# Attention, convolution and two MLPs on one core: scores made one unit ahead in the last groups, with six other moves of loads and fillers

## The chip, the cores and the metric

The kernel runs on 1 core of a Trainium2 chip, in one launch. The metric is the device time of that launch in microseconds (us), the median of several runs. Everything is in 32-bit floats.

## What is computed

The input is two images of 56 x 56 tokens with 384 channels. Two blocks follow one another; the reference, cut to what matters:

```python
# block 0: neighbourhood attention (12 heads of 32, 7 x 7 keys for each query), then an MLP
h = neighborhood_attention(layer_norm(x), w_qkv, b_qkv, rpb, w_proj, b_proj)
x = x + h
x = x + gelu(layer_norm(x) @ w1 + b1) @ w2 + b2            # 384 -> 1536 -> 384
# block 1: convolution and scans, then an MLP
p = layer_norm(x) @ w_in + b_in                            # 384 -> 768
local = conv3x3_depthwise(p)
mixed = 0.25 * (lr + rl + tb + bt) + local                 # four running means: decay 0.6, gain 0.4
x = x + layer_norm(mixed) @ w_out + b_out
x = x + gelu(layer_norm(x) @ w1 + b1) @ w2 + b2
```

The scores get a table of position biases (`rpb`) before the softmax, with a very negative value at every key outside a query's 7 x 7.

## The kernel before

**Engines and queues.** The order of the instructions is written out by hand, and each engine runs its own in that order. PE is TensorE, DVE VectorE, ACT ScalarE, POOL GpSimd. All transfers are issued by SP (`nc.sync`), in program order: an issue that has to wait for a semaphore holds all later ones.

**Start.** The first 448 tokens are loaded in four parts, normalized by DVE (L226), turned by PE (L357) and taken to SBUF by ACT (L362); then keys, values and queries are made (L386, L424). PSUM banks come from `any_bank`, four in turn.

**Attention.** The tokens lie in 14 groups of 8 rows (7 for an image), and a group in 4 windows of 14 columns (`Window`). A window's 12 heads are done in 3 units of 4 heads (`Unit`), so the loop has 168 steps `s`, 12 for a group (`n` is the group, `k` the step in it). The keys of a window are cut into 2 chunks at the image's edges (in the first and last group of an image, and in the first and last window of any) and into 3 elsewhere. For a unit with `m` chunks:

- `scores` (L515): 4 `m` matmuls, each recorded twice, into `sc`, two tiles of two banks, one bank for each head. A unit fills 112 `m` of a bank's 512 columns;
- `biased` (L530, DVE): adds the bias in two halves of two heads, from the banks to `pts`; `numerators` (L536, ACT) takes the exponential;
- `gathered` (L546, L548, DVE): adds the chunks for the sums, left out from group 12 on (`END`), where PE sums them instead;
- `values` (L556, L563): two steps later, values and sums into `o` and `sums`;
- for each window: `take` (L478, ACT), `gather` (L482), `invert` (L488 to L494) and `divide` (L498, L500).

Where two 2-chunk units follow one another, both are scored in one burst in the first one's step, the second at column 224, and nothing is scored in the second's step; else a unit is scored in its own step.

PE's time in a step is filled up with other matmuls, "fillers": queries, keys and values of later groups (`ahead`, L386 and L424) and projections of finished tokens (`project`, L582). A filler's bank is emptied at the start of the next step (`take` on ACT, or the add L590 on DVE). `spare` names the steps of a group that get no filler from `ahead`: 3, 4 and 5 where there are nine such jobs, which is so in group 11 (`END - 1`); that group gets no projections either. In groups 12 and 13 seven projections stand at steps written out in `THEN`; seven more come after the last unit.

**Loads of attention.** `Window` loads its values `vt` (L465) one window ahead. `load_bias` (L316) loads a table when the place changes, into one buffer for each of three kinds; 18 times in all. `load_residual` (L571) loads a tile of `x` for the residual into one of three `xr` buffers, so the load waits for the store of the tile three before; POOL adds the shift (L576), after `steps` steps or when the projection's add needs it. In the last 16 steps six parts of the first MLP's weights are loaded (L625), 768 KB each. At `s == NU`, behind the last unit, come the loads of the first two groups of `x1` (L609) and the last four residual tiles.

**MLPs and mixing** (`passes`). Block 0's MLP and block 1's input projection run group by group; `Beside` hands out convolution and scans on DVE in small steps between PE's work. Scans along the columns (`Columns`, one job for each image and channel block) add to `mix_d` in DRAM. The second pass (`dgroups`) loads a group of `mix_d` and `x2` (`load_mix`, L1274), measures it for the normalization during the hidden layer (`measure`, L1288: PE turns, DVE takes the statistics), and projects it out. `beside.until(name)` hands out DVE's jobs up to that one. Group 6 (`half_way`) is the first with tokens of image 1. Its load waits for the last job `(1, NI - 1)`, is cut into pieces of 128 tokens with all 6 channel blocks, and its tile `k` is measured in step 2 `k` + 3 of the 12 of the hidden layer (L1080) before.

Of the kernel before, what the change touches and what calls it, by code (L numbers as in the profile page):

```python
# [41 lines left out]
NH, KS, HD = 12, 7, 32  # L42
P = 128
NC = C // P
INNER, NI = 2 * C, 2 * C // P
HID, NHID = 4 * C, 4 * C // P
TT = 112
# [3 lines left out]
T1, T2 = H * W, B * H * W  # L51
# [122 lines left out]
def block_kernel(ctx: ExitStack, tc: tile.TileContext, ins: dict, out: bass.AP):  # L174
    nc = tc.nc
# [11 lines left out]
    mix_d = [dram.tile([NI, P, H * W], F32, name=f"mix_d{b}") for b in range(B)]  # L187
# [119 lines left out]
    def load_bias(n, j):  # L307

        b, g = groups_a[n]
        pr, pc = place(g, NG), place(j, NWC)  # L310
        if (b, pr, pc) in biases:
            return
        _, at, size = BIAS_T_AT[pr, pc]
        most = NH * TT * (3 if pc == 1 else 2)
        t = kp.tile([P, most], F32, name=f"bias{pc}")
        nc.sync.dma_start(out=t[:, :size], in_=ins["bias_t"][:, at : at + size])  # L316
        biases[b, pr, pc] = t[:, :size].rearrange("p (n c q) -> p n c q", n=NH, q=TT)

    load_x(0)
# [59 lines left out]
    def any_bank():  # L379

        return ps_s.tile([P, GT], F32, name="ps", tag="any")
# [186 lines left out]
    def load_residual(t, pool=lp, bufs=3, steps=4):  # L568

        xrs[t] = pool.tile([P, C], F32, name="xr", bufs=bufs)  # L570
        nc.sync.dma_start(out=xrs[t], in_=xf[t * P : (t + 1) * P, :])  # L571
        loaded[t] = steps
# [33 lines left out]
    def load_group(src, group, tag):  # L606
        t0, n = group
        t = xp.tile([P, NT, C], F32, name=tag)
        nc.sync.dma_start(  # L609
            out=t[:, :n, :], in_=src[t0 : t0 + n * P, :].rearrange("(k p) c -> p k c", p=P)  # L610
        )
        return t

    def weights(layer):

        w1 = wm.tile([P, NC, HID], F32, name=f"w1_{layer}", tag="w1")
        w2 = wm.tile([P, NHID, C], F32, name=f"w2_{layer}", tag="w2")
        s1 = ins[f"L{layer}_conv_w1"].rearrange("(c p) n -> p c n", p=P)
        s2 = ins[f"L{layer}_conv_w2"].rearrange("(c p) n -> p c n", p=P)
        parts = []  # L620
        for h in range(0, HID, HID // 3):
            parts.append((w1[:, :, h : h + HID // 3], s1[:, :, h : h + HID // 3]))
        for c in range(0, NHID, NHID // 3):
            parts.append((w2[:, c : c + NHID // 3, :], s2[:, c : c + NHID // 3, :]))
        return w1, w2, [lambda d=d, s=s: nc.sync.dma_start(out=d, in_=s) for d, s in parts]  # L625

    def norm_of(x, n, small):
        norm = Norm(small)
# [13 lines left out]
            nc.sync.dma_start(out=dst, in_=src)  # L642


    tps = [any_bank() for c in range(NC)]
    halves = [Norm(sm) for h in range(2)]
    for h, norm in enumerate(halves):
# [39 lines left out]
        channels_of(2, c, any_bank)()  # L687
    load_bias(0, 3)
    for t in range(3):
        load_residual(t)  # L690
    shift_by_values(ep, ps_t, wproj, shift)
    sctx.close()

# [13 lines left out]
    for s in range(NU + 4):  # L707
        n, k, hg, i = s // UG, s % UG, s % NC, s // NC
        if s == NU:

            kctx.close()
            xp = ctx.enter_context(tc.tile_pool(name="x", bufs=2, side="right", reuse_waits="tile"))
            tail_pool = actx.enter_context(tc.tile_pool(name="a_tail", bufs=1))
            xs = {g: load_group(x1f, groups[g], "xa") for g in range(2)}
            for t in range(T2 // P - 4, T2 // P):
                load_residual(t, tail_pool, 4, 2)
        store_all()
        while load:
            load_residual(load.pop(0))
        if k == 0 and n < ng:  # L720
            vals = []
            if n + 1 < ng:
                ahead += [lambda n=n, m=m: query_or_key(n + 1, m, one_bank) for m in range(NC)]
                vals += tiles_of(n + 1)[2:]
            if n + 2 < ng:
                vals += tiles_of(n + 2)[:2]
            ahead += [lambda t=t: value(t, one_bank) for t in vals]
            if n + 2 < ng:
                ahead += [
                    lambda n=n, m=m: query_or_key(n + 2, m, one_bank) for m in range(NC, 2 * NC)  # L730
                ]

            spare = (3, 4, 5) if len(ahead) == 9 else (4, 6)

        if k == 2 and n + 4 < ng:
            load_x(n + 4)
# [8 lines left out]
        if s < NU and hg == 2 and s + 1 < NU:  # L745
            ws[i + 1] = Window(i + 1)
        if s >= NU - UG - 4 and hg == 2 and w_parts:
            w_parts.pop(0)()

        if s <= NU:  # L750
            for take in taking:
# [5 lines left out]
        if s < NU:  # L757

            if s not in units:
                units[s] = Unit(ws[i], hg)  # L760
                units[s].scores()
                behind = Unit(ws[(s + 1) // NC], (s + 1) % NC) if s + 1 < NU else None
                if behind is not None and (units[s].m + behind.m) * TT <= BANK:
                    behind.scores(units[s].m)
                    units[s + 1] = behind
        new, before, last = units.get(s), units.get(s - 1), units.pop(s - 2, None)
        done = last.w if last is not None and last.hg == NC - 1 else None
# [203 lines left out]
    def passes(xs, xn, w1, w2, between=lambda ps: None):  # L971
# [14 lines left out]
        def images(t, n):  # L986


            for b in range(B):
                lo, hi = max(t, b * T1), min(t + n, (b + 1) * T1)  # L990
                if lo < hi:
                    yield b, lo - b * T1, lo - t, hi - lo
# [273 lines left out]
        def load_mix(g):  # L1266
            t0, n = dgroups[g]
            mx = io.tile([P, NI, MT], F32, name="mx")

            step = P if g == half_way else n * P  # L1270
            for t in range(0, n * P, step):
                for b, at, here, size in images(t0 + t, step):
                    here += t
                    nc.sync.dma_start(  # L1274
                        out=mx[:, :, here : here + size],
                        in_=mix_d[b][:, :, at : at + size].rearrange("m p t -> p m t"),
                    )
            x = load_group(x2_d, dgroups[g], "xa")
            if g >= half_way:
                add_row(x, dgroups[g][1], "b_out")  # L1280
            return mx, x, Norm(sm)

        def measure(mx, norm, k):
            parts = []
            for h in range(2):
                ps = ps_t.tile([P, NC, P], F32, name="xi", tag="pt")
                for c in range(NC):
                    nc.tensor.transpose(  # L1288
                        ps[:, c, :], mx[:, h * NC + c, k * P : (k + 1) * P], ident
                    )  # L1290
                parts.append(ps.rearrange("p c q -> p (c q)"))
            norm.add(k, parts)
# [12 lines left out]
        def measure_beside(m, g, ahead):  # L1305


            n = dgroups[g][1]
            if g > half_way:
                if m % 2 == 0 and m // 2 < n:  # L1310
                    measure_by_vector(ahead[0], ahead[2], m // 2)
            elif m % 2 == 1 and 0 < m // 2 <= n:
                measure(ahead[0], ahead[2], m // 2 - 1)
            if m == 10:
                ahead[2].close(n)

        def project_out(g, mx, x, inner):
# [174 lines left out]
        for g, (t0, n) in enumerate(dgroups):  # L1492
# [37 lines left out]
                    add_row(x3, dgroups[g + 1][1], "b2_1")  # L1530
                beside.go(ROW_D)
            if g + 2 == half_way:
                beside.until((1, NI - 1))
                ahead = load_mix(g + 2)
        pctx.close()

# [90 lines left out]
```

## Time and profile before

| | |
|---|---|
| median of 3 runs | 2680.19 us (2678.64 to 2681.08) |
| profiled execution | 2680.04 us, span 2678.2 us |
| PE busy | 2640.3 us (99%) |
| DVE busy | 1963.2 us (73%) |
| ACT busy | 898.7 us (34%) |
| POOL busy | 249.7 us (9%) |
| DMA | 299 MB, mean 112 GB/s |
| PE idle in 0 to 20 us | 7.46 us |
| PE idle in 570 to 710 us | 14.1 us |
| PE idle in 2110 to 2140 us | 7.66 us |

Times in the profile are from the span's start. A group of the profile reads: line, engine, operation, output<-inputs, count, busy time, and the idle time before it with what ended it. Ends of matmuls are modelled, so a stall within a burst shows as a longer burst. "PEclk" is the share of TensorE's full clock that was granted.

### The profile page before, as it was taken

What the parts mean: (1) busy time and instruction counts of PE and PEld (TensorE: products, weight loads), DVE (VectorE), ACT (ScalarE), POOL (GpSimd) and SP (SyncE); (2) the same over time, 40 slices, a digit from 0 to 9 for tenths busy, and PEclk for the clock granted to TensorE, in tenths of its full rate; (3) what the DMA queues carried; (4) which work ended last, traced back from release to release, by engine and by line L of the source; (5) the groups of instructions that cost most, each with busy time, mean ns of one, the idle gap of its engine ahead of it and who ended that gap; (6) DMA issues with size and microseconds to landing.
All of it is one profiled execution on the core that took longest, in us unless ns stands there. A gap on an engine that the chain in (4) does not pass through costs nothing. (4 is left out here: it accounts for less than half of the span.)

```text
span 2678.2 us, 37275 instructions
## 1 busy us (share of the span) xinstructions
PE 2640.3 (99%) x14963; PEld 1473.9 (55%) x14963; DVE 1963.2 (73%) x3539; ACT 898.7 (34%) x1447; POOL 249.7 (9%) x264
## 2 busy tenths in 40 slices
PE   8999999999899999999999999999999899999999
PEld 4666666656655455555555555555555455555556
DVE  3778877876365698688989889888988627677652
ACT  4555555554322332223344422311143211111111
POOL 1111111111211100000010000000010011101100
PEclk9999999999999999999999999999999999999999
DMA  6323454224411132233346544533346401111000
GB/s 216 134 89 102 154 170 146 80 77 158 156 37 38 65 107 88 89 128 105 123 156 230 184 149 150 178 120 114 118 182 228 152 19 37 45 44 39 30 12 17
DMA packets 134249, 298.99 MB, mean 112 GB/s; under 512 B 11463, under 2 KB 89905, under 8 KB 131761
## 3 DMA queue, kind: packets, MB, share of 16 engines
q1 hardware_dynamic: 134064, 296.50, 32.3%
q8 instruction: 119, 1.95, 0.3%
q14 instruction: 66, 0.53, 0.1%
HBM read 180.86 MB, written 115.61 MB: 111 GB/s over the span
## 5 line engine op out<-in xcount | busy, mean ns | idle before, releaser
L1080 PE MATMUL mm<-hT,w 128*128 128x512 f32 (+2 forms) x1872 | 771.1, 569 | 0.4 <-ACT hT L254 0.2
L1080 PEld LDWEIGHTS mm<-hT,w 128*128 128x128 f32 x1872 | 352.7, 190 | 383.5 <-issue 352.1
L1089 ACT ACTIVATE hid<-mm,chan 128x512 f32<-128x512 f32 (+2 forms) x312 | 206.1, 661 | 683.3 <-PE mm L1080 683.2
L1096 PE MATMUL y_end<-w,hid 128*128 128x384 f32 x1200 | 395.2, 486 | 0.0
L1174 DVE SCALAR_TENSOR_TENSOR loc<-pt,taps,loc 128x990 f32<-128x990 f32 (+9 forms) x336 | 377.1, 1122 | 10.0 <-ACT loc L1156 1.7
L1096 PE MATMUL y<-w,hid 128*128 128x384 f32 x1152 | 379.4, 486 | 0.0
L1096 PEld LDWEIGHTS y_end<-w,hid 128*128 128x128 f32 x1200 | 227.5, 190 | 157.2
L1096 PEld LDWEIGHTS y<-w,hid 128*128 128x128 f32 x1152 | 218.2, 190 | 150.5 <-issue 1.0
L530 DVE TENSOR_TENSOR pts<-sc,bias 119x448 f32<-119x448 f32 (+3 forms) x336 | 220.9, 699 | 78.2 <-PE sc L515 75.2
L536 ACT ACTIVATE pts<-pts 119x448 f32<-119x448 f32 (+3 forms) x336 | 206.8, 642 | 191.3 <-DVE pts L530 187.9
L222 POOL TENSOR_TENSOR rs<-rs,mhalf 128x4 f32<-128x4 f32 (+4 forms) x67 | 87.1, 1300 | 1727.0 <-DVE rs L219 1691.6
L386 PE MATMUL ps<-hT,wqkv 128*128 128x448 f32 x504 | 212.0, 559 | 2.0 <-ACT qT L396 0.7
L1064 DVE STREAM_TRANSPOSE hT<-xn 32x96 f32<-32x96 f32 x672 | 181.1, 269 | 31.4 <-PE mm L1080 11.8
L1080 PE MATMUL mm<-hT,w_in 128*128 128x512 f32 (+2 forms) x468 | 191.9, 568 | 0.6 <-ACT hT L254 0.6
L240 ACT ACTIVATE xn<-xc,sh,rs 128x384 f32<-128x384 f32 x98 | 64.7, 698 | 268.6 <-DVE sh L233 268.5
L1080 PEld LDWEIGHTS mm<-hT,w_in 128*128 128x128 f32 x468 | 88.5, 190 | 102.1 <-issue 90.6
L386 PEld LDWEIGHTS ps<-hT,wqkv 128*128 128x128 f32 x504 | 90.2, 191 | 82.8 <-issue 73.1
L515 PEld LDWEIGHTS sc<-qT,kT 32*100 32x100 f32 (+3 forms) x3168 | 91.6, 170 | 67.1 <-issue 17.9
L1299 DVE STREAM_TRANSPOSE turned<-mx 32x192 f32<-32x192 f32 x336 | 123.3, 367 | 4.2
L515 PE MATMUL sc<-qT,kT 32*100 32x112 f32 (+3 forms) x3168 | 114.7, 272 | 6.5 <-DVE pts L530 5.8
L556 PE MATMUL o<-pts,vt 100*32 100x112 f32 (+3 forms) x3168 | 112.7, 266 | 3.8 <-DMA vt<-v_d 2.7
L582 PE MATMUL ps<-wproj,og 128*128 128x384 f32 x294 | 107.1, 503 | 3.6 <-DVE xr L590 3.6
(104 smaller groups left out, 2644.9 us busy)
## 6 DMA issues: line engine op xcount, KB each, us to landing
bias<-in_bias_t SPq DMA_DIRECT2D x16, 1344.0 KB
loc<-loc_d SPq DMA_DIRECT2D x24, 784.0 KB
mixed<-mix_d SPq DMA_DIRECT2D x24, 784.0 KB
mix_d<-mixed SPq DMA_DIRECT2D x24, 784.0 KB
xa<-x_d SPq DMA_DIRECT2D x22, 768.0 KB
p_d<-mx SPq DMA_DIRECT2D x10, 1536.0 KB
mx<-mix_d SPq DMA_DIRECT2D x10, 1536.0 KB
pt<-p_d SPq DMA_DIRECT2D x18, 560.0 KB
```

The costliest lines, as they stand in the source:

```text
L386: nc.tensor.matmul(ps, lhsT=wqkv[:, c, m * P : (m + 1) * P], rhs=hT[:, c, half_of(n)], start=c == 0, stop=c == NC - 1,)
L515: nc.tensor.matmul(sc[i // 2][: w.keys, i % 2, (first + c) * TT : (first + c + 1) * TT], lhsT=kT[d, hg, w.keys_at + r * w.kc : w.keys_at + ...
L530: nc.vector.tensor_tensor(self.of(half), sc[half][:n, :, at].rearrange("p h (c q) -> p h c q", q=TT), self.w.bias[:n, 4 * self.hg + h : 4 ...
L536: nc.scalar.activation(self.of(half), self.of(half), AF.Exp)
L556: nc.tensor.matmul(o[i * HD : (i + 1) * HD, hg, :], lhsT=w.vt[:n, c, h * HD : (h + 1) * HD], rhs=self.pts[:n, i, c, :], start=c == 0, stop ...
L582: nc.tensor.matmul(ps, lhsT=ogs[t // 7][:, c, at : at + P], rhs=wproj[:, c, :], start=c == 0, stop=c == NC - 1,)
L1064: nc.vector.transpose(hT[j : j + HD, :, k * P + i : k * P + i + HD], xn[i : i + HD, k, :].rearrange("p (c q) -> p c q", c=NC)[:, :, j : j ...
L1080: nc.tensor.matmul(ps[:, : n * P], lhsT=w[:, c, m * P : (m + 1) * P], rhs=hT[:, c, : n * P], start=c == 0, stop=c == NC - 1,)
L1089: nc.scalar.activation(t[:, : n * P], ps[:, : n * P], AF.Gelu, bias=col(b1, m))
L1096: nc.tensor.matmul(ps, lhsT=t[:, k * P : (k + 1) * P], rhs=w[:, m, :], start=m == 0, stop=m == len(lhs) - 1,)
L1174: nc.vector.scalar_tensor_tensor(to, pt[:, lo + dy - self.top : hi + dy - self.top, xt : xt + n], self.tap(dy, dx), to, ALU.mult, ALU.add,)
L1299: nc.vector.transpose(t[j : j + HD].rearrange("p (m c) -> p m c", m=NI)[:, :, i : i + HD], mx[i : i + HD, :, k * P + j : k * P + j + HD],)
```

## The change

- Bias tables of all groups but the first are issued by ACT (`nc.scalar`) instead of SP, and so are the six parts of the first MLP's weights.
- Twelve matmuls of `ident` stand at PE's start; their result is not used.
- The first three residual tiles get their shift after 8 steps instead of 4.
- At `s == NU` two residual tiles come ahead of each of the two groups of `x1`, which were first.
- In group 11 `spare` is (3, 6, 9).
- From group 12 on, a step whose unit has its scores makes those of the next one, in the half of the banks that its own unit does not take (where both have 2 chunks).
- The half-way group's mixture is loaded in two parts: five channel blocks once the last but one job is done, the sixth after the last. Its tiles are measured two steps later, and its statistics closed at step 11 instead of 10.

```diff
@@ -313,7 +313,8 @@
         _, at, size = BIAS_T_AT[pr, pc]
         most = NH * TT * (3 if pc == 1 else 2)
         t = kp.tile([P, most], F32, name=f"bias{pc}")
-        nc.sync.dma_start(out=t[:, :size], in_=ins["bias_t"][:, at : at + size])
+        queue = nc.sync if n == 0 else nc.scalar
+        queue.dma_start(out=t[:, :size], in_=ins["bias_t"][:, at : at + size])
         biases[b, pr, pc] = t[:, :size].rearrange("p (n c q) -> p n c q", n=NH, q=TT)
 
     load_x(0)
@@ -622,7 +623,7 @@
             parts.append((w1[:, :, h : h + HID // 3], s1[:, :, h : h + HID // 3]))
         for c in range(0, NHID, NHID // 3):
             parts.append((w2[:, c : c + NHID // 3, :], s2[:, c : c + NHID // 3, :]))
-        return w1, w2, [lambda d=d, s=s: nc.sync.dma_start(out=d, in_=s) for d, s in parts]
+        return w1, w2, [lambda q=nc.sync, d=d, s=s: q.dma_start(out=d, in_=s) for d, s in parts]
 
     def norm_of(x, n, small):
         norm = Norm(small)
@@ -642,6 +643,10 @@
             nc.sync.dma_start(out=dst, in_=src)
 
 
+
+    warm = any_bank()
+    for _ in range(12):
+        nc.tensor.matmul(warm[:HD, :P], lhsT=ones_hd, rhs=ident, start=True, stop=True)
     tps = [any_bank() for c in range(NC)]
     halves = [Norm(sm) for h in range(2)]
     for h, norm in enumerate(halves):
@@ -687,7 +692,7 @@
         channels_of(2, c, any_bank)()
     load_bias(0, 3)
     for t in range(3):
-        load_residual(t)
+        load_residual(t, steps=8)
     shift_by_values(ep, ps_t, wproj, shift)
     sctx.close()
 
@@ -711,9 +716,11 @@
             kctx.close()
             xp = ctx.enter_context(tc.tile_pool(name="x", bufs=2, side="right", reuse_waits="tile"))
             tail_pool = actx.enter_context(tc.tile_pool(name="a_tail", bufs=1))
-            xs = {g: load_group(x1f, groups[g], "xa") for g in range(2)}
-            for t in range(T2 // P - 4, T2 // P):
-                load_residual(t, tail_pool, 4, 2)
+            xs = {}
+            for g in range(2):
+                for t in range(T2 // P - 4 + 2 * g, T2 // P - 2 + 2 * g):
+                    load_residual(t, tail_pool, 4, 2)
+                xs[g] = load_group(x1f, groups[g], "xa")
         store_all()
         while load:
             load_residual(load.pop(0))
@@ -731,6 +738,8 @@
                 ]
 
             spare = (3, 4, 5) if len(ahead) == 9 else (4, 6)
+            if n == END - 1:
+                spare = (3, 6, 9)
 
         if k == 2 and n + 4 < ng:
             load_x(n + 4)
@@ -745,7 +754,8 @@
         if s < NU and hg == 2 and s + 1 < NU:
             ws[i + 1] = Window(i + 1)
         if s >= NU - UG - 4 and hg == 2 and w_parts:
-            w_parts.pop(0)()
+
+            w_parts.pop(0)(nc.scalar)
 
         if s <= NU:
             for take in taking:
@@ -759,9 +769,17 @@
             if s not in units:
                 units[s] = Unit(ws[i], hg)
                 units[s].scores()
-                behind = Unit(ws[(s + 1) // NC], (s + 1) % NC) if s + 1 < NU else None
-                if behind is not None and (units[s].m + behind.m) * TT <= BANK:
+                paired = True
+            else:
+
+                paired = n >= END
+            behind = Unit(ws[(s + 1) // NC], (s + 1) % NC) if paired and s + 1 < NU else None
+            if behind is not None and (units[s].m + behind.m) * TT <= BANK:
+                if units[s].first == 0:
                     behind.scores(units[s].m)
+                    units[s + 1] = behind
+                elif behind.m * TT <= units[s].first:
+                    behind.scores()
                     units[s + 1] = behind
         new, before, last = units.get(s), units.get(s - 1), units.pop(s - 2, None)
         done = last.w if last is not None and last.hg == NC - 1 else None
@@ -1267,14 +1285,21 @@
             t0, n = dgroups[g]
             mx = io.tile([P, NI, MT], F32, name="mx")
 
-            step = P if g == half_way else n * P
-            for t in range(0, n * P, step):
-                for b, at, here, size in images(t0 + t, step):
-                    here += t
+            def load_channels(lo, hi):
+                for b, at, here, size in images(t0, n * P):
                     nc.sync.dma_start(
-                        out=mx[:, :, here : here + size],
-                        in_=mix_d[b][:, :, at : at + size].rearrange("m p t -> p m t"),
+                        out=mx[:, lo:hi, here : here + size],
+                        in_=mix_d[b][lo:hi, :, at : at + size].rearrange("m p t -> p m t"),
                     )
+
+            if g == half_way:
+
+                beside.until((1, NI - 2))
+                load_channels(0, NI - 1)
+                beside.until((1, NI - 1))
+                load_channels(NI - 1, NI)
+            else:
+                load_channels(0, NI)
             x = load_group(x2_d, dgroups[g], "xa")
             if g >= half_way:
                 add_row(x, dgroups[g][1], "b_out")
@@ -1309,9 +1334,12 @@
             if g > half_way:
                 if m % 2 == 0 and m // 2 < n:
                     measure_by_vector(ahead[0], ahead[2], m // 2)
-            elif m % 2 == 1 and 0 < m // 2 <= n:
-                measure(ahead[0], ahead[2], m // 2 - 1)
-            if m == 10:
+            else:
+                late = 2 if g == half_way else 0
+                k = (m - late) // 2 - 1
+                if m % 2 == 1 and 0 <= k < n:
+                    measure(ahead[0], ahead[2], k)
+            if m == (NHID - 1 if g == half_way else 10):
                 ahead[2].close(n)
 
         def project_out(g, mx, x, inner):
@@ -1530,7 +1558,6 @@
                     add_row(x3, dgroups[g + 1][1], "b2_1")
                 beside.go(ROW_D)
             if g + 2 == half_way:
-                beside.until((1, NI - 1))
                 ahead = load_mix(g + 2)
         pctx.close()
 
```

## The prediction

> **What bounds the kernel now.** I read the page first, then the waits of PE, the granted clock by windows, and the timelines around each wait.
>
> ```profile
> span 2678.2 us, 37275 instructions
> PE 2640.3 (99%) x14963; PEld 1473.9 (55%) x14963; DVE 1963.2 (73%) x3539; ACT 898.7 (34%) x1447; POOL 249.7 (9%) x264
> ```
>
> PE is busy in all but 37.9 us, and the change takes no matmul away (it adds 12). So it can give back only PE's waits, the time lost in them to a lower clock, and stalls inside bursts. The waits of PE:
>
> ```profile
> PE xi L1288 <- DMA mx<-mix_d: 7.7, 1, 7.7
> PE ps L357 <- DVE xg L226: 7.0, 1, 7.0
> PE sc L515 <- DVE pts L530: 5.8, 10, 1.3
> PE ps L582 <- DVE xr L590: 3.6, 2, 2.6
> PE o L556 <- DMA vt<-v_d: 2.7, 2, 2.4
> PE sums L563 <- DVE sum L546: 1.2, 1, 1.2
> ```
>
> Columns: total us, times, longest. All but the second (the first data's arrival) is touched by the change. The windows in which the clock was halved (PEclk is third from the end) each follow one of these waits:
>
> ```profile
> 583.87:590.70 6.83, 6.83 (x62) 4.00 (x58) 4.35 (x8) 2.12 (x4) 0.00 (x0) 0.50 0.00 0
> 655.55:658.96 3.41, 3.41 (x28) 2.02 (x18) 1.30 (x3) 1.38 (x3) 1.16 (x2) 0.50 0.43 157
> 679.44:682.85 3.41, 3.41 (x81) 3.20 (x78) 1.77 (x4) 1.05 (x2) 0.00 (x0) 0.50 0.28 71
> 2130.10:2136.90 6.80, 4.38 (x10) 2.69 (x11) 1.34 (x3) 0.00 (x0) 0.00 (x0) 0.50 1.18 309
> ```
>
> PE's busy time at half clock is half lost: 3.4, 1.7, 1.7 and 2.2 us. Attention's last two groups run from about 609 to 689 us, its last projections to 707 us.
>
> **What the Trainium skill says.** "TensorE: Matmul & The Clock Gate", Part 1: the clock is half until a window of some 3.4 us was busy, and drops after an idle one. The trace agrees: the stretches are 3.41 us or twice that. It is milder than "idle": 1.35 us of wait plus a stalled burst (652 to 655.5) was enough. "PSUM — Partial Sum Buffer", PSUM bank collisions: two engines may not touch one bank and quadrant at once, at any columns. So the free half of a bank does not let PE write beside DVE's read. The trace agrees: the first bias add of the pair of score units at 605.97 starts at 607.10, when the whole pair (1.10 us) is done. "DMA: Bandwidth & Descriptors", Issuing engines are not separate DMA queues: another issuing engine saves only issue time. Here that is not all, since a waiting issue holds those queued behind it (below).
>
> **The change part by part**, against the profiled run of 2680.04 us (span 2678.2; the median of the runs is 2680.19).
>
> *Warm-up matmuls.* 12 matmuls of 128 columns. A 448-column record at half clock takes 0.75 us, so 24 records take 24 x 0.214 = 5.1 us, from 1.6 us (ones_hd is set) to 6.7, before PE's first transpose at 7.02: hidden in that 7.0 us wait. Worth:
>
> ```profile
> 9.96 8.94 PE L386 MATMUL ps<-hT,wqkv 128*128 128x448 f32 x18 [0.44 <-ACT hT L362]
> 25.70 6.94 PE L386 MATMUL ps<-hT,wqkv 128*128 128x448 f32 x18
> ```
>
> The same 18 records cost 2.0 us more at first, and the transposes before them (2.50 against 1.31) some 0.5. But PE waits again for DVE and ACT between, and the clock may drop once more. Bounds 0.6 and 2.4; **1.8 us**.
>
> *Residual adds at step 8 rather than 4.* POOL's three adds (2.90 us from 63.56) lie ahead of the copy to `wide`, and beside them a 0.31 us DVE pair grew to 1.75:
>
> ```profile
> 63.78 1.75 DVE L492 SCALAR_TENSOR_TENSOR good<-totals,good 128x11 f32<-128x11 f32 x2
> ```
>
> PE then lost 0.19 + 1.17 us and 0.5 in a stalled burst (L515, 66.12). At step 8 POOL has just finished a window. The adds may slow DVE there, under a filler matmul. Bounds 0 and 1.9; **1.2 us**.
>
> *Idle filler slots (3,6,9) instead of (3,4,5) in group 11.* Three units without filler in a row, 574.8 to 583.5, cost 2.3 us of waits on L530, then 6.83 us of half clock (3.4):
>
> ```profile
> 582.71 0.44 PE L515 MATMUL sc<-qT,kT 32*100 32x112 f32 x4 [1.12 <-DVE pts L530]
> ```
>
> A three-chunk unit gives DVE 1.62 + 1.23 us and some 0.7 of window work, PE 2.0 without filler and 4.2 with. Alone, a slot costs one stall of about 0.4 and DVE catches up in the next. So 2.3 + 3.4 - 3 x 0.4 = 4.5. Bounds 2.5 and 5.5; **4.4 us**.
>
> *Bias tables and the first layer's weights issued by ACT.* 15 of 18 tables and 6 weight parts leave SP. What this removes is seen on SP:
>
> ```profile
> SPq L571 <- DMA x_d<-xr: 38.4, 7, 8.8
> SPq L625 <- DMA v_d<-vs: 2.0, 1, 2.0
> ```
>
> A residual load waits for the store of the tile before; that store lies behind 1344 KB of table and 768 KB of weights (661.44 issued, load let go at 670.78), and behind the load waits the values' load `vt`. PE's 2.4 + 0.3 us for `vt` go, and the half clock at 679 (1.7). On ACT, 21 issues of about 0.4 us are 8.4 us of an engine busy 34%. Queued behind each are bank evacuations and exponentials. The tables' buffers were last read by adds that ACT's own exponentials have already followed, so ACT waits for none; the first weight part waits for `v_d` until 636.4, about when ACT gets there. I take 0 there.
>
> *Scores one unit ahead.* Before, two units are scored at once, and the next pair waits for both units' adds, which sit behind the projection's add (L590), itself waiting for PE:
>
> ```profile
> 653.64 1.54 PE L515 MATMUL sc<-qT,kT 32*102 32x112 f32 x32 [1.35 <-DVE pts L530]
> 661.46 1.62 PE L515 MATMUL sc<-qT,kT 32*120 32x112 f32 x32 [0.70 <-DVE pts L530]
> ```
>
> After a filler DVE needs 0.56 + 0.35 + 1.15 = 2.1 us, PE has 1.0 of other work. From 640 to 689 such gaps are 1.35 + 0.70 + 0.94 = 3.0, stalls inside six bursts (1.55 to 1.65 instead of 1.10) 2.8, the half clock at 655 1.7. After, a score waits for the add of one unit earlier, done before the filler ended. Not free: by bank, the add still waits for the score just issued. Without filler a cycle is 0.6 + 0.1 + 1.15 = 1.85 to 2.1 us, PE's work 1.7: some 0.3 in each of 8 steps, and 0.6 at the last unit. Score part: 3.0 + 2.8 + 1.7 - 3.0 = 4.5; with `vt` 2.7 and its clock 1.7, **8.6 us** (rounded down from 8.9). Bounds 4 and 10.
>
> *Order of the last loads.* The third late add waits:
>
> ```profile
> 704.15 0.56 DVE L590 TENSOR_TENSOR xr<-ps,xr 128x384 f32<-128x384 f32 x1 [5.71 <-POOL xr L576]
> 704.77 2.20 PE L582 MATMUL ps<-wproj,og 128*128 128x384 f32 x6 [2.59 <-DVE xr L590]
> ```
>
> Its load is issued at 700.53, when a store issued at 694.06 behind 768 KB of weights and 1728 KB of groups and residuals has landed. With the weights earlier on ACT and SP less held, it should be issued about 697 and added about 700.6. Seven projections of 2.1 us from 689.0 then end at 703.8 instead of 706.97. Bounds 1 and 3.6; **3.2 us**.
>
> *Half-way mixture in two loads, measured two steps later.* DVE ends the last channel at 2124.0; PE waits to 2132.52. Now, five of six channels load at about 2116, beside the hidden layer. After the last store lands (the first half let a load go at 2126.55), one channel of 256 KB: 0.4 us issue and about 2 us to land, 2129. PE asks at step 5, not 3: 2114.4 + 6 x 2.58 = 2129.9. The wait of 7.7 goes, and 2.2 of clock. The statistics close after step 11, about 3 us before a use that two projections of 4 us cover. **10.0 us**; bounds 7.5 and 10.3.
>
> Sum: 1.8 + 1.2 + 4.4 + 8.6 + 3.2 + 10.0 = 29.2. 2680.04 - 29.2 = 2650.8, on the median's scale (+0.15) 2651.0.
>
> **The rivals.** (1) *The waits come back elsewhere*: the last channel is still late, the projections stay behind the shared DMA engines, the clock drops at the spread slots. Taking the lower bounds, 0.6 + 0 + 2.5 + 4 + 1 + 7.5 = 15.6: 2664. For: DMA moves 375 GB/s from 694 to 698 whatever the queue. Against: from 80 to 570 us, with the same units and transfers, PE is idle 0.46 us in all. (2) *Scores ahead do nothing*, since banks are shared: minus the score part of 4.5, 2655. For: the add at 607.10. Against: the order of waits above. (3) *Slower: ACT held at its DMA issues.* If each of the 21 holds exponentials and evacuations on PE's path, the gain is gone at 29.2/21 = 1.4 us each; at 1.9 (the longest `mx` issue on SP) it is 2651 + 40 = 2691. For: a weights issue took 1.31 at 689.34, and PE did wait for ACT's evacuations (0.72, 0.28). Against: the median table issue is 0.37 us, and ACT mostly waits for PE or DVE.
>
> **How the numbers follow.** A difference of 0.2%, about what a measurement of this kernel can tell, is 5.4 us. Forecast 0.66, (1) 0.18, (2) 0.06, (3) 0.07, and 0.03 for a loss that eats most of the gain. The first three are faster, save a rest of 0.02: faster 0.88, same 0.05, slower 0.07. Range: the forecast's parts at their upper bounds together give 33.7 us, 2646; downward it takes in (1) with a margin: 2644 to 2667.
>
> **What would show it.** Right: no PE wait on `mx` or `vt`; no half clock at 580 to 690 and 2130; score bursts of 16 records with L530 waits of 0.3 us or less in the last groups; L1080 starting some 20 us earlier than 708.78; the first 18 L386 near 6.9 us. Wrong: PE waiting for ACT (L396, L411) at new places, table issues on ACT of over 1 us, or the wait at L1288 merely shorter.

## The result and the profile after

| | before | after |
|---|---|---|
| median | 2680.64 us (2678.64 to 2681.68, 4 runs) | 2663.32 us (2660.36 to 2666.79, 4 runs) |
| ratio, 95% interval | | 0.9937 (0.992 to 0.9954) |
| profiled execution, span | 2680.04, 2678.24 us | 2666.79, 2664.99 us |

The kernel became 17.3 us faster, not 29. The profiled execution is the slowest of its four and 13.25 us shorter than that of before. The page of after:

```profile
span 2665.0 us, 37316 instructions
PE 2642.1 (99%) x14987; PEld 1476.7 (55%) x14987; DVE 1962.1 (74%) x3539; ACT 898.5 (34%) x1447; POOL 250.0 (9%) x264
```

PE has 24 records more (the 12 warm-up matmuls) and is idle 22.9 us where it was idle 37.9. Its waits (us in total, times, longest):

```profile
PE ps L387 <- ACT vs L432: 4.5, 3, 2.4
PE sc L516 <- DVE pts L531: 2.0, 5, 0.8
PE ps L358 <- ACT xg L240: 1.9, 4, 1.1
PE ps L649 <- DVE ones_hd L292: 1.7, 1, 1.7
```

The waits for `mx`, `vt`, the projection's add and most of the time lost to L530 (now L531) are gone. On top stands one that before did not have: PE waits for ACT's copies of the values. Two of the stretches at half clock (PEclk, third from the end) follow it, at new places; the last groups and the half-way group have none:

```profile
27.77:34.60 6.83, 6.08 (x8) 2.87 (x9) 0.54 (x1) 2.97 (x5) 0.00 (x0) 0.50 0.80 212
324.73:328.14 3.41, 3.41 (x8) 1.52 (x7) 0.62 (x1) 1.02 (x3) 0.00 (x0) 0.50 0.97 318
578.00:690.00 112.00, 106.55 (x1955) 69.80 (x1948) 79.92 (x167) 53.97 (x98) 13.26 (x29) 1.00 0.44 146
2100.00:2140.00 40.00, 40.00 (x125) 20.99 (x124) 22.62 (x27) 8.99 (x13) 3.43 (x1) 1.00 0.63 222
```

The two traces laid side by side by PE's own landmarks say where the time went. A stretch ends at the first value matmul (L556, after: L557) of a unit ("the last" is the last record of that line), at the first matmul of the MLP (L1080, L1098), or behind the 1860th record of that line, which lies behind the half-way group. Worked out from the times of the records, in us:

| stretch of PE's work | before | after | change |
|---|---|---|---|
| start to unit 0 | 53.96 | 59.87 | +5.91 |
| units 0 to 12 | 42.38 | 41.11 | -1.27 |
| units 12 to 66 | 214.88 | 214.88 | 0.00 |
| units 66 to 78 | 47.86 | 52.00 | +4.14 |
| units 78 to 130 | 204.92 | 205.55 | +0.63 |
| units 130 to 144 (group 11) | 53.87 | 49.82 | -4.05 |
| unit 144 to the last (groups 12, 13) | 70.56 | 66.64 | -3.92 |
| last unit to the first MLP | 20.35 | 16.49 | -3.86 |
| MLPs and mixing to the 1860th record | 1507.23 | 1497.21 | -10.02 |
| the rest | 462.24 | 461.41 | -0.83 |

Six stretches gain some 24 us, and 10.7 are given back: 5.9 at the start and 4.8 between units 66 and 130, where the prediction had put a small gain and nothing.

### The profile page after: what moved, and what is told of

The parts are those of the page before. It is cut to its first block, busy times and chain, and to the rows that moved or that the text cites. A ratio compares the mean times of both kernels' runs of the same rounds, so it can differ in the third digit from the quotient of the medians.

```text
span 2665.0 us, 37316 instructions
## 1 busy us (share of the span) xinstructions
PE 2642.1 (99%) x14987; PEld 1476.7 (55%) x14987; DVE 1962.1 (74%) x3539; ACT 898.5 (34%) x1447; POOL 250.0 (9%) x264
## 5 line engine op out<-in xcount | busy, mean ns | idle before, releaser
L1098 PE MATMUL mm<-hT,w 128*128 128x512 f32 (+2 forms) x1872 | 769.4, 569 | 0.4 <-ACT hT L254 0.2
L1098 PEld LDWEIGHTS mm<-hT,w 128*128 128x128 f32 x1872 | 352.8, 190 | 382.2 <-issue 350.8
L531 DVE TENSOR_TENSOR pts<-sc,bias 119x448 f32<-119x448 f32 (+3 forms) x336 | 221.1, 700 | 72.4 <-PE sc L516 67.6
L1098 PE MATMUL mm<-hT,w_in 128*128 128x512 f32 (+2 forms) x468 | 191.9, 569 | 0.6 <-ACT hT L254 0.6
L1098 PEld LDWEIGHTS mm<-hT,w_in 128*128 128x128 f32 x468 | 88.7, 190 | 101.9 <-issue 90.4
L557 PE MATMUL o<-pts,vt 100*32 100x112 f32 (+3 forms) x3168 | 111.0, 264 | 1.6 <-ACT og L479 1.0
L425 PE MATMUL ps<-wqkv,hT 128*128 128x384 f32 x294 | 106.9, 502 | 0.0
```

Source lines behind the costliest of these rows:

```text
L425: nc.tensor.matmul(ps, lhsT=hT[:, c, at : at + P], rhs=wqkv[:, c, 2 * C :], start=c == 0, stop=c == NC - 1,)
L531: nc.vector.tensor_tensor(self.of(half), sc[half][:n, :, at].rearrange("p h (c q) -> p h c q", q=TT), self.w.bias[:n, 4 * self.hg + h : 4 ...
L557: nc.tensor.matmul(o[i * HD : (i + 1) * HD, hg, :], lhsT=w.vt[:n, c, h * HD : (h + 1) * HD], rhs=self.pts[:n, i, c, :], start=c == 0, stop ...
L1098: nc.tensor.matmul(ps[:, : n * P], lhsT=w[:, c, m * P : (m + 1) * P], rhs=hT[:, c, : n * P], start=c == 0, stop=c == NC - 1,)
```

## The experiments

All times are medians; each kernel was timed beside runs of the kernel before on its own chip (2680.34 us for e1 to e4, 2681.49 for e5 to e8 and again for e9 to e11, three chips), so a difference of medians across chips can be off by 1.2 us. A ratio's interval is some 3.6 us to either side. Many differences below are no larger than that: there the stretches of the profiles carry the argument.

| kernel | us (range) | ratio to before (95%) |
|---|---|---|
| e1_again: the changed kernel, unaltered | 2663.45 (2660.01 to 2663.85) | 0.993 (0.9917 to 0.9944) |
| e2_pairs | 2662.58 (2659.46 to 2666.53) | 0.9933 (0.992 to 0.9947) |
| e3_no_warm | 2665.92 (2662.85 to 2670.18) | 0.995 (0.9937 to 0.9964) |
| e4_tables_sp | 2659.05 (2657.59 to 2660.39) | 0.9919 (0.9906 to 0.9933) |
| e5_half_way_back | 2666.58 (2665.34 to 2674.76) | 0.9956 (0.9941 to 0.997) |
| e6_x_early | 2657.11 (2656.02 to 2658.93) | 0.9913 (0.99 to 0.9926) |
| e7_fillers | 2667.12 (2661.99 to 2673.15) | 0.9948 (0.9936 to 0.996) |
| e8_weights_sp | 2664.95 (2659.76 to 2666.9) | 0.9936 (0.9922 to 0.9951) |
| e9_x_pairs | 2658.04 (2657.1 to 2660.76) | 0.9916 (0.9902 to 0.9929) |
| e10_vs3 | 2655.17 (2654.21 to 2656.14) | 0.9903 (0.9888 to 0.9919) |
| e11_act_tables_vs3 | 2659.35 (2657.4 to 2664.39) | 0.9922 (0.9908 to 0.9935) |

Stretches of their profiled executions, in us, cut as above:

| | start to unit 0 | 66 to 130 | 130 to 144 | 144 to last | last to MLP | to 1860th | rest |
|---|---|---|---|---|---|---|---|
| before | 53.96 | 252.78 | 53.87 | 70.56 | 20.35 | 1507.23 | 462.24 |
| after | 59.87 | 257.55 | 49.82 | 66.64 | 16.49 | 1497.21 | 461.41 |
| e1_again | 57.69 | 256.78 | 49.82 | 66.63 | 16.51 | 1497.20 | 461.41 |
| e2_pairs | 55.94 | 257.14 | 49.98 | 65.94 | 17.10 | 1497.20 | 461.42 |
| e3_no_warm | 54.96 | 258.53 | 49.83 | 66.82 | 16.24 | 1497.24 | 461.41 |
| e4_tables_sp | 55.08 | 252.78 | 49.84 | 66.63 | 16.95 | 1497.23 | 461.45 |
| e5_half_way_back | 53.45 | 252.77 | 49.82 | 67.52 | 16.99 | 1505.41 | 462.35 |
| e6_x_early | 53.73 | 252.77 | 49.83 | 66.73 | 16.50 | 1497.21 | 461.44 |
| e7_fillers | 58.82 | 252.77 | 49.99 | 76.13 | 16.79 | 1497.20 | 461.45 |
| e8_weights_sp | 55.20 | 252.78 | 49.83 | 72.50 | 17.90 | 1497.23 | 461.44 |
| e9_x_pairs | 53.95 | 252.77 | 49.98 | 67.51 | 16.89 | 1497.18 | 461.87 |
| e10_vs3 | 51.64 | 252.79 | 49.83 | 67.98 | 16.88 | 1497.21 | 461.44 |
| e11_act_tables_vs3 | 56.18 | 252.77 | 49.83 | 66.64 | 17.29 | 1497.20 | 461.41 |

### e1_again: is the loss between units 66 and 130 there every time?

No edit: the changed kernel, profiled once more.

> The changed kernel once more, unaltered. Its profile lost 5.9 us up to the first score burst (52.22 against 46.31 us) and 4.1 us near 321 us. Theory A (the change moved the bound at the start to the load of the second 448 tokens, and the tables on ACT's queue hold stores): both losses repeat, first score burst at 50 to 53 us, a wait of PE for L432 of 2 us or more near 320, time 2661 to 2667. Theory B (both are the luck of one execution's transfers): the first score burst stands near 44.5 to 47 us or the wait at 320 is gone, and the time is 2655 to 2662.

The same 4 us come back (256.78, and again in e2 and e3), with the wait for `vs` and 3.41 us of half clock at 321 us. So this loss belongs to the kernel. The start differs from one execution to the next, 57.69 against 59.87; of the 4.8 us lost between units 66 and 130 in the profile of after, 0.8 is not in this one. All other stretches agree within 0.02.

### e4_tables_sp and e11_act_tables_vs3: the bias tables on ACT

e4 puts the tables back on SP; the weights stay on ACT.

```diff
-        queue = nc.sync if n == 0 else nc.scalar
+        queue = nc.sync
```

> The changed kernel with all bias tables issued by SP again; the weights stay on ACT. The prediction gives the tables on ACT no cost and no gain before group 12, and together with the weights 4.4 us at 660 to 683 (vt and a half clock): so 0 to 3 us more. Rival (tables on a second queue cost PE 2.4 us of waiting for L432 and 1.7 us of clock near 321 us): 2 to 4 us less.

4.4 us faster than e1_again, on the rival's side and not on that of the prediction's step. Units 66 to 130 take 252.78 us, to a hundredth what they took before, and PE's wait there and the half clock after it are gone. So moving the tables cost all of that stretch. Why, SP's timeline shows. Before, then after:

```profile
290.13 0.34 SPq L316 DMA_DIRECT2D bias<-in_bias_t  x1
296.43 0.33 SPq L642 DMA_DIRECT2D x_d<-xr  x1
299.38 0.33 SPq L571 DMA_DIRECT2D xr<-in_x  x1
...
311.12 0.38 SPq L642 DMA_DIRECT2D v_d<-vs  x1
```

```profile
301.08 0.33 SPq L643 DMA_DIRECT2D x_d<-xr  x1
307.21 0.34 SPq L572 DMA_DIRECT2D xr<-in_x  x1
...
320.46 0.37 SPq L643 DMA_DIRECT2D v_d<-vs  x1
```

and ACT's, after:

```profile
300.09 0.33 ACTq L317 DMA_DIRECT2D bias<-in_bias_t  x1
...
323.15 0.48 ACT L432 COPY vs<-ps 128x384 f32<-128x384 f32 x1 [4.63 <-DMA v_d<-vs]
```

and PE's, after:

```profile
323.69 3.85 PE L387 MATMUL ps<-hT,wqkv 128*128 128x448 f32 x6 [2.39 <-ACT vs L432]
```

SP has nothing to compute, so it had issued the table at 290.13, ahead of the loop's other engines. ACT issues it when it gets there. The times of the two fences can't be compared as they stand: after is 4.65 us late here, because its start took longer. Counted back from the first values of unit 66, the table was issued 21.1 us ahead by SP and 15.8 us ahead by ACT, 5.3 us later, while the residual's store stands at 14.8 us in both: the table is now 1.0 us ahead of that store, where it was 6.3. The `xr` load, which waits for that store to land, then follows it by 6.1 us instead of 2.95. Load and store take turns three times in that stretch, and behind them in SP's queue stands the store of the values (`v_d<-vs`): 320.46, by the same count 4.7 us later than before. In every profile with tables on ACT that first gap of store and load is 6.0 to 6.9 us, in every one with them on SP 2.3 to 3.0. With two buffers for `vs`, ACT's third copy waits for that store; PE's next filler waits for the bank that this copy empties.

e11 keeps the tables on ACT and takes away only the last link:

```diff
-            vs = ep.tile([P, C], F32, name="vs", bufs=2)
+            vs = ep.tile([P, C], F32, name="vs", bufs=3)
```

> The changed kernel with its tables on ACT, and three buffers for the values in place of two. Theory (the later table delays the residual's store and load on SP, SP's queue holds the values' store behind them, ACT's third copy waits for its buffer, and PE for ACT): the copy at 323 us no longer waits, PE's 2.4 us and the half clock there go, the stretch of units 66 to 78 falls from 52.0 to 48 or 49 us, and the whole to 2658 to 2660; what may be left is 1.5 us in the stretch of units 78 to 130. Rival (ACT loses the time to its own DMA issues): the stretch stays at 51 to 52 us and the whole at 2663.

2659.35 us, and 252.77 us for units 66 to 130. SP's queue is as late as in after (first fence: SP, second: ACT), and nobody waits for it:

```profile
297.62 0.33 SPq L643 DMA_DIRECT2D x_d<-xr  x1
303.74 0.34 SPq L572 DMA_DIRECT2D xr<-in_x  x1
...
316.19 0.37 SPq L643 DMA_DIRECT2D v_d<-vs  x1
```

```profile
315.55 0.48 ACT L432 COPY vs<-ps 128x384 f32<-128x384 f32 x1 [0.49 <-PE ps L425]
```

Store and load are 6.1 us apart again, but the third copy comes ahead of the values' store and waits for PE alone. The rival, that ACT loses the time to its own issues, falls: the issues are the same 15, of 0.33 to 0.38 us each.

### e3_no_warm, e6_x_early and e10_vs3: the start

e3 leaves out the 12 matmuls.

```diff
-    warm = any_bank()
-    for _ in range(12):
-        nc.tensor.matmul(warm[:HD, :P], lhsT=ones_hd, rhs=ident, start=True, stop=True)
```

> The changed kernel without the twelve warm-up matmuls. The prediction's step gives it 1.8 us more. Rival (the second 448 tokens land too late, so PE's faster start ends in a wait, and that wait drops the clock): 0 to 4 us less than the changed kernel, with no half clock between 25 and 35 us.

2665.92 against 2663.45 us, with ranges that overlap by 1 us, and so do the intervals of the ratios: by the medians the warm-up is worth some 2.5 us, but that is not clear of the noise. The profile does not show it: the stretch to unit 0 took 54.96 us without the matmuls and 53.45 to 59.87 with them, in the kernels that load `xg` as after does. The execution profiled was the fastest of e3's five, so what the slower ones lost was not seen. PE's timeline of after shows the gain and how it is lost:

```profile
1.73 5.30 PE L649 MATMUL ps<-ident,ones_hd 128*32 128x128 f32 x24 [1.73 <-DVE ones_hd L292]
...
9.96 7.03 PE L387 MATMUL ps<-hT,wqkv 128*128 128x448 f32 x18 [0.62 <-ACT hT L363]
...
28.52 10.04 PE L387 MATMUL ps<-hT,wqkv 128*128 128x448 f32 x18 [1.50 <-ACT vs L432]
```

The first 18 records are 1.9 us faster than before, and PE is early. But the second group's tokens landed at 18.84 us in this execution (15.47 before), ACT normalizes them late, its value copies stand behind that, and its third copy waits for the first one's store. PE waits 1.09, three times 0.28, and 1.50 us, and the clock drops: the second 18 records take 10.04 instead of 6.94.

What sets the start can be read from all the profiles that load these tokens as after does, counted from the moment at which DVE begins on them. With the warm-up and the clock kept full, unit 0 follows 38.02 us later in each of e4, e5 and e8, whose tokens came at 17.06, 15.43 and 17.18 us. In e3, without the warm-up, they came at 16.92, and unit 0 followed 38.04 us later. Where the clock dropped again it was more: 39.48 us (e1), 39.72 (e2), 40.34 (e7) and 41.03 (after). So in these executions the start was the landing of the tokens plus 38 us, with the warm-up or without it, and 1.5 to 3.0 us more where the clock fell. Before and e5 are the fairest pair: their tokens came at 15.47 and 15.43 us, and the start took 53.96 us without and 53.45 with the warm-up, 0.5 us less.

e6, on top of e4, loads the second group's tokens ahead of the query third of the weights:

```diff
+        if i == 0:
+            load_x(1)
...
-    load_x(1)
```

> e4 with the second 448 tokens loaded ahead of the query weights. Theory (in the changed kernel these tokens land at 16.2 to 18.8 us, so ACT normalizes them late, its value copies are late and the third waits for the first one's store; PE waits 1.5 us and more, and with it the warm-up's gain goes): first score burst 2 to 3.5 us earlier than in e4 (47.4 us), no wait of PE for ACT between 20 and 30 us, time 2 to 3 us less. Rival (the start is bound by something else, ACT's own work or the weights): within 1 us of e4.

2657.11 us, 1.9 less than e4 (on another chip; against before 0.9913 and 0.9919, within the noise). In the profile the tokens come 2.7 us earlier than in e4 (14.40 against 17.06), but the first score burst only 1.35 us earlier (46.08), less than the 2 to 3.5 expected. As in e4's profile the clock stays full in the start, and PE's second keys take 7.03 us; the wait for ACT that was to go is still there:

```profile
25.37 7.03 PE L388 MATMUL ps<-hT,wqkv 128*128 128x448 f32 x18 [1.56 <-ACT vs L433]
```

These are 1.56 us for ACT's third copy. e10 gives `vs` three buffers on top of e6 (the edit of e11):

> The same early load with scores ahead, and three buffers in place of two for the values on their way to memory (vs). Theory: PE's wait of 1.6 us for ACT's third copy of values at 25 us goes, since that copy no longer waits for the first copy's store; the piece up to the first unit falls by 1 to 1.6 us from 53.7, the rest stays: 2655.5 to 2656.5. Rival (ACT is late there for the normalization, not for the buffer): the wait stays under another name, 2657.

That wait goes, and the start takes 51.64 us, 2.3 less than before: about all that the prediction thought the warm-up could give, now that the tokens and the buffer are there in time. It is partly given back: PE, earlier now, waits 2.7 us for `vt` in the last groups (67.98 us instead of 66.73). 2655.17 us is the fastest of all these kernels, 0.9903 of before and 8.2 us faster than the changed kernel.

### e2_pairs and e9_x_pairs: the scores made one unit ahead

Both score the last groups in pairs, as before; e2 on the changed kernel, e9 on e6.

```diff
-                paired = n >= END
+                paired = False
```

> The changed kernel with scores made in pairs again in the last two groups; all else of the change stays. The prediction's step gives it 4.5 us more than the changed kernel. Rival (a bank is shared, so each score burst of a step without filler waits for both halves of one add: bursts of 1.16 to 1.21 instead of 0.64 to 0.69 us, nine times, in the changed profile): between 2 us less and 1.5 us more, with bursts of 32 at 1.5 us and L531 gaps of 1.35 and 0.70 back.

> Tables issued by SP, the second group's tokens loaded ahead of the query third of the weights, and the last two groups scored in pairs as before. It asks once more what the scores made one unit ahead are worth, now beside 2657.1 us without the pairs. Theory (the scores of one unit ahead wait for the add that reads the same banks, so they only move the stalls): 2656 to 2658, the stretch from unit 144 to the last within 1 us of 45.4 us. Rival (the first comparison, 0.9 us, hid a gain behind the waits of the tables on ACT): slower by 3 to 4.5 us, 2660.5 to 2661.5, with waits for the adds of 3 us and more in that stretch.

e2 was 0.9 us faster than e1_again, e9 0.9 us slower than e6. In the stretch of the last groups the pairs took 65.94 against 66.63 us, and 67.51 against 66.73. Timed, the signs differ and the ranges overlap, so making the scores ahead is worth nothing that these runs can tell. The profiles show where e2 and e9 part: in both, a pair waits 1.34 us for the adds, and in e9 the clock is then halved for a window at 649 us, as it was before at 655, while in e2 it stays full; and two later pairs wait 1.24 and 0.70 us in e9, 0.14 and 0.34 in e2. Both ways stall, in different places. With the scores ahead (after), PE waits before one burst only, but every burst that has no filler before it is stretched:

```profile
662.93 0.69 PE L516 MATMUL sc<-qT,kT 32*120 32x112 f32 x16
664.61 1.20 PE L516 MATMUL sc<-qT,kT 32*120 32x112 f32 x16
666.74 1.20 PE L516 MATMUL sc<-qT,kT 32*120 32x112 f32 x16
```

Seven bursts of the last groups (not nine, as the expectation has it) take 1.16 to 1.21 us instead of 0.64 to 0.69: 7 x 0.52 = 3.6 us, and there are waits of 0.77 us (before a burst) and 0.54 (for an exponential). With pairs (e9) the bursts of 32 are stretched and PE waits before four of them, 4.0 us in all:

```profile
656.23 1.62 PE L517 MATMUL sc<-qT,kT 32*120 32x112 f32 x32 [0.70 <-DVE pts L532]
661.58 1.11 PE L517 MATMUL sc<-qT,kT 32*120 32x112 f32 x32
```

### e8_weights_sp: the first MLP's weights on SP again

On top of e4.

```diff
-            w_parts.pop(0)(nc.scalar)
+            w_parts.pop(0)(nc.sync)
```

> e4 with the six weight parts on SP as well, so that no load is left on ACT's queue. The prediction's step: 4.4 us more (vt's waits of 2.7 us and a half clock of 1.7 at 675 to 683 come back), and some of the last projections' 3.2 us. Rival (scores ahead and the new order at the end already take SP off the path): under 1 us more.

5.9 us slower than e4 (on another chip; 0.9936 and 0.9919 of before): the last groups take 72.50 instead of 66.63 us, and the tail 0.95 more. The wait for `vt` is back, twice as long as before:

```profile
PE o L557 <- DMA vt<-v_d: 5.8, 5, 2.3
```

and with it two stretches of half clock, 3.41 us each, at 666.6 and 683.7. So of the two things moved to ACT, the weights carry the gain and the tables the loss.

### e5_half_way_back: the half-way load as before

On top of e4, with the load in pieces of 128 tokens, the wait for the last job, and the measuring at the old steps:

```diff
-            if g == half_way:
-                beside.until((1, NI - 2))
-                load_channels(0, NI - 1)
-                beside.until((1, NI - 1))
-                load_channels(NI - 1, NI)
...
             if g + 2 == half_way:
+                beside.until((1, NI - 1))
                 ahead = load_mix(g + 2)
```

> The changed kernel with the tables on SP (e4, 2659.05 us), and the half-way mixture loaded and measured as before the change. The prediction's step: 10.0 us more than e4, all of it in the MLPs, with PE's wait of 7 to 8 us on mx and 6.8 us of half clock near 2110 us back. Rival (the MLPs' gain in the changed kernel came from another part, such as earlier weights): under 3 us more.

7.5 us slower than e4 (on another chip; 0.9956 and 0.9919 of before). In the profile the stretch to the 1860th record grows by 8.18 us and the rest by 0.90, and the wait is back, with 6.83 us of half clock behind it:

```profile
PE xi L1306 <- DMA mx<-mix_d: 6.4, 1, 6.4
```

The load in two parts and the later measuring were undone together; what each is worth alone was not run.

### e7_fillers: the projections of the last groups, more evenly spread

On top of e4, with pairs:

```diff
-    END, THEN = ng - 2, (7, 9, 11, 13, 16, 19, 22)
+    END, THEN = ng - 2, (7, 10, 12, 14, 16, 18, 20)
```

> e4 with scores in pairs again and the seven projections of the last two groups at steps 7, 10, 12, 14, 16, 18, 20 instead of 7, 9, 11, 13, 16, 19, 22, so that nearly each pair has its filler in the second unit's step. Theory (the waits before a pair come from a filler just ahead of the add that the pair waits for): the stretch from unit 150's values to attention's last (45.28 us with scores ahead, 44.59 with pairs) falls to 41 to 43 us, 2 to 3 us less in all. Rival (these waits are DVE's load, wherever the fillers stand): within 1 us of e4.

8.1 us slower than e4 rather than faster (on another chip; 0.9948 and 0.9919 of before, six runs from 2661.99 to 2673.15); the last groups take 76.13 us in the execution profiled, one of the slower ones. Pairs alone don't do that: with the old steps that stretch took 65.94 (e2) and 67.51 us (e9). The projections also pace SP's queue. Counted from unit 0 on (e7 gets there 3.7 us later), the second projection's store is issued 1.3 us later than in e4, the load behind it 3.6, and the next store 3.3. The load behind this store is let go after 8.5 us, in e4 after 4.25 (648.14 to 652.39): now a table and a weight part have been issued just ahead of it. And behind that load stand the values of the last window but two, 7.1 us later than in e4 (653.62) by the same count (SP, then PE):

```profile
655.15 0.36 SPq L643 DMA_DIRECT2D x_d<-xr  x1
663.68 0.33 SPq L572 DMA_DIRECT2D xr<-in_x  x1
664.45 1.52 SPq L466 DMA_DIRECT2D vt<-v_d  x2
```

```profile
668.78 0.60 PE L557 MATMUL o<-pts,vt 120*32 120x112 f32 x8 [5.84 <-DMA vt<-v_d]
```

PE waits four times for `vt`, 10.4 us, and in two stretches of half clock, 6.83 us each, its 4.54 and 5.12 us of busy time lose half, 4.8 us.

## Why the prediction came out as it did

The forecast was 2651.0 us and the measurement 2663.3: faster, inside the range, and at the figure of rival (1), 2664. That agreement is chance. None of the three waits that (1) named came back: PE did not wait for the last channel, the late projections ran without a gap, and the clock stayed full at the spread slots. Four of the terms came out nearly as priced, scores ahead and weights gave 4.7 us less than forecast, and two losses that neither the forecast nor (1) had priced took some 11 us back. By the forecast's own steps:

| step | predicted | measured, from the stretches |
|---|---|---|
| warm-up | 1.8 | -5.9 (after), -3.7 (e1) |
| residual adds at step 8 | 1.2 | 1.3 |
| spare (3, 6, 9) | 4.4 | 4.05 |
| tables on ACT | 0 | -4.8 (after), -4.0 (e1); timed -4.4 |
| weights on ACT and scores ahead | 8.6 | 3.9 |
| order of the last loads | 3.2 | 3.9 |
| half-way load | 10.0 | 10.0, and 0.8 later |
| sum | 29.2 | 13.3 (after) |

**The half-way load** went as worked out. PE asks for the tile at the step named, and it is there:

```profile
2112.00 15.61 PE L1098 MATMUL mm<-hT,w 128*128 128x512 f32 x36
2127.45 0.82 PE L1313 MATMUL xi<-ident,mx 128*128 128x128 f32 x6
```

The five channels were issued at 2113.22, the last after 2121.73. e5 undid this part and lost 7.5 us timed, 9.1 in the profile.

**Spare, residual adds, last loads** came within 0.7 us each. None of the three was undone by itself: each figure is that of the stretch in which the edit stands. In group 11 the waits for L531 are 0.23 and 0.33 us and the clock stays full. The seven late projections run without a gap:

```profile
690.46 14.11 PE L583 MATMUL ps<-wproj,og 128*128 128x384 f32 x42
```

though one of the adds still waits 4.85 us for POOL, at 701.75: PE has other banks by then. This term contains some of the weights: with them on SP the tail is 0.95 us longer (e8).

**Tables on ACT** is the step that failed. It priced the issues at 0.4 us each on an idle engine and asked whether ACT would have to wait at them. That was right: 15 issues of 0.33 us in the median, none over 0.38, and rival (3) did not happen. What the step left out is when ACT gets to its issue: 5.3 us later in PE's work than SP did, just ahead of a store on which SP's queue depends. e4 undoes it (4.4 us), and e11 shows the chain's last link. This loss of 4.0 to 4.8 us stands where the step had put nothing. One of the signs named for a wrong forecast, PE waiting for ACT at new places, is what the profile shows, though at L432 and not at L396 or L411.

**Scores ahead** was mis-sized: 4.5 us were forecast, and two comparisons gave -0.9 and +0.9. Rival (2) had this mechanism. "Some 0.3 in each of 8 steps" was 0.52 in seven bursts and 1.3 in two waits, 4.9 us in place of 3.0; and of the 7.5 us set against it the 1.7 of clock were there in only one of the two executions with pairs. The weights alone made good the other half: predicted 4.4 (`vt` and its clock), measured by e8 5.9 timed, against the kernel with scores ahead. Stretches of the last groups: 70.56 before, 65.94 with the weights moved and pairs kept (e2), 66.64 with both.

**Warm-up** saved its 1.9 us in the first 18 records, and the way in which it might be lost was named ("PE waits again for DVE and ACT between, and the clock may drop once more"), but bounded at 0.6 of gain. What the term left out is how little slack the next supplier had: the start ended 38 us after the second group's tokens landed, so with tokens at 15.4 us only 0.5 of the 1.8 was to be had (e5 against before), and with later tokens nothing, or less where the clock fell. In every profile with the tokens loaded as in after the start took between 0.5 us less and 5.9 more than before. Of the 5.9 in after, 3.0 are the clock that dropped again; the rest is the landing, 3.4 us later than before, less the 0.5 won. e6 and e10 show that the gain is there once the tokens come earlier and `vs` has a third buffer: 53.7 and 51.6 us. Why the landing differs from one execution to the next stays open, and so does the median of e3, 2.5 us slower without the warm-up, which the one profile of e3 does not show.

The sign that L1080 would start some 20 us earlier failed too: it was 2.4 us. The stretches before it gained 13.1 and lost 10.7. Of the other signs for right, the bursts of 16 came, with one wait of 0.77 us where 0.3 was the limit.

**Clock, queues and banks.** Of the Trainium skill's three statements in the prediction, "TensorE: Matmul & The Clock Gate", Part 1, has the clock drop after an idle window of some 3.4 us. The half-clock stretches are again 3.41 us or twice that, but a wait of 2.39 us was enough for one (after, at 324.73), less than an idle window. "DMA: Bandwidth & Descriptors", Issuing engines are not separate DMA queues, says that another issuing engine saves only the time of issue, which it calls small. Here it changed two larger things: the moment of issue, by 5.3 us of PE's work, and what waits behind it; 15 tables cost 4.4 us and six weight parts brought 5.9. "PSUM — Partial Sum Buffer", PSUM bank collisions, has two engines kept apart by bank and quadrant of partitions, whatever the columns. The stretched bursts (1.16 to 1.21 us) agree with a program that keeps PE and DVE apart by bank; a version with other banks was not run, so that the banks are the cause is argued.

## What to carry to other kernels

A transfer moved to another engine's queue is issued when that engine reaches it in its program, not when the old queue did: look at what then shares the DMA engines with it, and follow the first queue's waiting issues to whoever has too few buffers. An edit that makes one engine earlier, a warm-up or a filler, pays only if the next supplier has slack; price the next wait with the lost clock behind it. Undo the parts of a bundle one at a time: here two edits of the same kind, tables and weights to ACT, had opposite signs.

## What the runs showed of the hardware

A load that waits for a 192 KB store was issued 2.95 us after the store where the last table, of 1344 KB, had been issued 6.3 us ahead of the store (before), 6.1 us after it where such a table was issued 1.0 us ahead (after, e11), and 8.5 us with 768 KB of weights and 1344 KB of table ahead (e7, weights at 653.53 and table at 653.91, store at 655.15). DVE could begin on the second group's tokens at 15.4 to 18.8 us with the same transfers queued ahead of them, and that difference between executions, 3.4 us, is as large as most edits of this study.
